# Deformable convolution by halves: 4x4 sampling tiles on the two row halves of TensorE in place of 7x7 tiles on its four column groups

## The chip, the core and the metric

The kernel runs on one core of a Trainium2 chip. The metric is the device time of one execution in microseconds, the median of several runs. Engines are called by the profile's names: PE is TensorE (PEld its weight loads), DVE is VectorE, ACT is ScalarE, POOL is GpSimd, SP is SyncE, which here only issues DMAs.

## The reference

The input is 32 images of 96 channels, 56 x 56, float32. Two layers follow each other. The first is an inverted bottleneck: a 1x1 convolution to 576 channels, a depthwise 3x3 convolution, a squeeze-and-excitation gate, a 1x1 projection back to 96 channels and the residual. The second computes attention over channels and positions from Fourier magnitudes (twice), a gate, an ordinary 3x3 convolution and a deformable 3x3 convolution, and normalises over the whole batch. The part that the change is about:

```python
y = x * ca * sa
offset = _conv(aux, off_w, off_b, (1, 1))          # 18 channels: 9 taps, x and y
gate = sigmoid(_conv(relu(_conv(aux, dg1_w, ...)), dg2_w, dg2_b))
y_base = _conv(y, base_w, base_b, (1, 1))
off = offset.reshape(b, 9, 2, h, w)
px = xx + off[:, :, 0]
py = yy + off[:, :, 1]
sampled = _grid_sample_taps(y, px, py)             # bilinear, 9 samples a position
y_def = einsum('bcthw,oct->bohw', sampled, def_w) + def_b
z = (1 - gate) * y_base + gate * y_def
zn = batch_norm(z)                                 # mean and variance over the batch
out = relu(zn + x)
```

## The kernel before

All 32 images go through both layers in one software pipeline (`layers`). While the main loop works on the deformable part of image b, two generators ("streams") are stepped beside it: `attend` of image b+1 (projection, Fourier transforms, attention) and `hidden` of image b+2 (the 1x1 and depthwise convolutions, the latter nine VectorE instructions a unit at line 223). `pump()` counts slots, and steps each stream as often as its share of the slots is due; things that wait are put in `later` with a slot number. The framework's scheduler then orders the instructions on each engine at build time; on SP the order is that of the program text. [...]

The main loop goes over bands of rows. Before, a band is 7 rows (`TR`), 8 bands an image, 256 in all, and a band is 8 sampling tiles of 7 x 7 positions (`TP` = 49). Sampling is done as a matmul: offsets reach at most 2 pixels (`REACH`), so a tile's samples come from a window of 11 x 11 = 121 pixels (`NS`), and the samples of all channels are the window's pixels (channels as the stationary operand, transposed to 121 partitions) times a matrix of bilinear weights, 121 x 441 (9 taps x 49 positions). Should an offset be larger, `gather_block` does everything again by gathering; it does not run on this input.

For each band the steps, with their lines, are:

- `offsets` (a generator, run two bands ahead, one `next` a slot): the joint convolution (L540: hidden gate, offsets and 32 base channels in one), ACT moves `off` out (L585), the base convolution for the other 64 channels (L569, two halves of the columns side by side) and its sum on DVE (L572); DVE takes the largest offset `top` (L591), POOL adds the place in the window (L593) and stores `od` to DRAM (L595); SP loads it back repeated as `ht` (L600); ACT and DVE make one-dimensional hat weights of it (L603, L605); POOL stores them as `hd` (L609).
- `weights_load` (L617, L619): SP loads column weights `wc` and row weights `wr` for two tiles, repeated over the window's partitions; `weights` (L625): DVE multiplies them. `AHEAD` and `READY` set how far ahead.
- `block_pixels` (L633): POOL copies the 8 windows `ybl` of the next band; `block_channels` (L643, L645): PE transposes each to 121 partitions, ACT copies it out as `yt`.
- `sample_tile` (L654, L660, L662): per tile, three matmuls of 32 channels each over the first 7 taps (343 columns) to partitions 0-31, 32-63, 64-95, and three for the last two taps to partitions 96-127, packed so that a later matmul can use all 128 rows; ACT copies the whole 128 x 343 to `v`.
- `gate_of` (L677), `deform` (L669): 7 matmuls over a band's 392 positions, the first on 96 rows, the other six on 128 (a full tap and a third of one of the last two taps); `combine` (L695 to L698) on DVE mixes with the base convolution; `store` (L945) on POOL.

Of the streams, the change touches the projection: `project_loads` (L271, L274) issues five `hq` loads and one residual load `xc` on POOL for a band of 7 rows, `project` (L283, L285) multiplies them. PSUM is 7 banks in a shared pool `mm` and one, `acc`, for small things.

Of the kernel before, what the change touches and what calls it, by code (L numbers as in the profile page):

```python
# [19 lines left out]
NCH = 5  # L20
# [10 lines left out]
TR = 7  # L31
NBD = H // TR
NTX = W // TR
TP = TR * TR
BW = TR * W
REACH = PD
SB = TR + 2 * REACH
# [5 lines left out]
VC = KA * TP  # L43
# [6 lines left out]
GP = 98  # L50
# [7 lines left out]
AHEAD = 2  # L58
READY = 2
# [84 lines left out]
def expand(nc, p, xts, unit):  # L144
# [23 lines left out]
    if half is None:  # L168
        nc.vector.memset(h1[:64, 0, :], 0.0)
        nc.vector.memset(h1[64:, HH + 1, :], 0.0)  # L170
        for r in range(1, HH + 1, TR):
            piece([(0, 0), (64, 1)], r, TR)
            yield
        piece([(0, 0)], HH + 1, 1)
        piece([(64, 1)], 0, 1)
        yield
    else:
        r = 1 - half
        for rows in (TR + 1, TR, TR, TR):
            piece([(0, half)], r, rows)  # L180
            r += rows
            yield
# [80 lines left out]
def project_loads(nc, p, x, h2d, q):  # L263

    half, n0 = divmod(q * BW, HB)
    terms = [(u, ch, slice(0, 128)) for u, (ch, hf) in enumerate(UNITS) if hf == half]
    terms.append((4, 4, slice(64 * half, 64 * half + 64)))
    rows = []
    for u, ch, ps in terms:
        hq = p["hq"].tile([128, BW], FP, name="hq")  # L270
        nc.gpsimd.dma_start(hq[ps], h2d[u, ps, n0 : n0 + BW])  # L271
        rows.append((ch, ps, hq))
    xr = p["xc"].tile([C, BW], FP, name="xc")
    nc.gpsimd.dma_start(xr, x[:, q * TR : (q + 1) * TR].rearrange("c h w -> c (h w)"))  # L274
    return rows, xr


def project(nc, p, rows):
# [3 lines left out]
    for i, (ch, ps, hq) in enumerate(rows):  # L282
        nc.tensor.matmul(pt[:C, :BW], w3s[ps, ch], hq[ps], start=(i == 0), stop=(i == NCH - 1))  # L283
    o = p["o"].tile([C, BW], FP, name="o")
    nc.scalar.activation(o, pt[:C, :BW], AF.Identity, bias=w["sh3"], scale=w["inv3"])  # L285
# [97 lines left out]
def attend(tc, p, b, x, h2d, pooled, x1, given=False):  # L383
# [7 lines left out]
    if not given:  # L391
        yield from squeeze(nc, p, pooled)
        rows, xr = project_loads(nc, p, x, h2d, 0)
        for _ in range(2):
            yield
        for q in range(NBD):
            o = project(nc, p, rows)
            yield
            nc.gpsimd.tensor_tensor(o, o, xr, ALU.add)
            nc.gpsimd.dma_start(x1[:, q * BW : (q + 1) * BW], o)  # L400
            if q + 1 < NBD:
                rows, xr = project_loads(nc, p, x, h2d, q + 1)
            yield
# [112 lines left out]
def load_rows(nc, p, yp, b, x1, r0, r1):  # L516
# [3 lines left out]
    sab = p["q2"].tile([C, TR, W], FP, name="sab")[:, : r1 - r0]  # L520
# [13 lines left out]
def conv3(nc, out, weights, yp, channels, j):  # L534

    view = out.rearrange("p (h w) -> p h w", h=TR)
    for k in range(NTAP):
        dy, dx = divmod(k, 3)
        r0 = j * TR + dy + PD - 1
        nc.tensor.matmul(view, weights[:, k], yp[:channels, r0 : r0 + TR, dx + PD - 1 : dx + PD - 1 + W],  # L540
# [13 lines left out]
def joint_conv(nc, p, yp, j):  # L554
# [11 lines left out]
    for k in range(NTAP):  # L566
        dy, dx = divmod(k, 3)
        r0 = j * TR + dy + PD - 1
        nc.tensor.matmul(pb[k % 2 * BC : (k % 2 + 1) * BC, :BW].rearrange("p (h w) -> p h w", h=TR), w["base"][:, k],  # L569
                         yp[:C, r0 : r0 + TR, dx + PD - 1 : dx + PD - 1 + W], start=(k < 2), stop=(k > NTAP - 3))  # L570
    nc.scalar.activation(yb[:BC], pb[:BC, :BW], AF.Identity, bias=w["cv"]("base_b")[:BC])
    nc.vector.tensor_tensor(yb[:BC], yb[:BC], pb[BC:, :BW], ALU.add)  # L572


def offsets(nc, p, yp, j, top, hids, ybs, hds):
# [8 lines left out]
    off = p["off"].tile([NOFF, NTX, TP], FP, name="off")  # L584
    nc.scalar.activation(off.rearrange("o t (r c) -> o t r c", r=TR),  # L585
                         pa.rearrange("o (r t c) -> o t r c", r=TR, t=NTX), AF.Identity, bias=w["offc"])
    yield
    for _ in joint:
        pass
    flat = off.rearrange("o t p -> o (t p)")  # L590
    nc.vector.tensor_reduce(top, flat, AX.X, ALU.max, apply_absolute_value=True)  # L591
    yield
    nc.gpsimd.tensor_tensor(off, off, w["place"].unsqueeze(1).to_broadcast([NOFF, NTX, TP]), ALU.add)  # L593
    od = p["dp"].tile([NTX, NOFF, TP], FP, name="od")
    nc.gpsimd.dma_start(od.rearrange("t o p -> o t p"), off)  # L595
    yield
    yield
    ht = p["ht"].tile([NTX * SB, 2 * KP], FP, name="ht")
    src = od.rearrange("t o p -> t (o p)").unsqueeze(1).to_broadcast([NTX, SB, 2 * KP])
    nc.sync.dma_start(ht, src)  # L600
    yield
    yield
    nc.scalar.activation(ht, ht, AF.Abs, bias=w["blk"])  # L603
# [3 lines left out]
    hd = p["dp"].tile([SB, 2, NTX, KP], FP, name="hd")  # L607
    for x in range(2):
        nc.gpsimd.dma_start(hd[:, x].rearrange("i t n -> t i n"), ht[:, x * KP : (x + 1) * KP])  # L609
# [3 lines left out]
def weights_load(nc, p, hd, m):  # L613

    src = hd.rearrange("i x t n -> i x (t n)")[:, :, 2 * m * KP : 2 * (m + 1) * KP]
    wc = p["wc"].tile([NS, 2 * KP], FP, name="wc")
    nc.sync.dma_start(wc, src[:, 0].unsqueeze(0).to_broadcast([SB, SB, 2 * KP]))  # L617
    wr = p["wr"].tile([NS, 2 * KP], FP, name="wr")
    nc.sync.dma_start(wr, src[:, 1].unsqueeze(1).to_broadcast([SB, SB, 2 * KP]))  # L619
# [9 lines left out]
def block_pixels(nc, p, yp, j):  # L629

    yb = p["ybl"].tile([C, NTX, SB, SB], FP, name="ybl")
    for t in range(NTX):
        nc.gpsimd.tensor_copy(yb[:, t], yp[:C, j * TR : j * TR + SB, t * TR : t * TR + SB])  # L633
    return yb


def block_channels(nc, p, yb):

    yt = p["yt"].tile([128, NTX, C], FP, name="yt")
    for i in range(0, NTX, 4):  # L640
        pt = bank(p)
        for t in range(4):
            nc.tensor.transpose(pt[:NS, t * C : (t + 1) * C], yb[:, i + t].rearrange("c r x -> c (r x)"),  # L643
                                p["w"]["ident"][:C, :C])
        nc.scalar.copy(yt[:NS, i : i + 4].rearrange("p t c -> p (t c)"), pt[:NS, : 4 * C])  # L645
# [3 lines left out]
def sample_tile(nc, p, yt, s, v, n):  # L649


    ps = bank(p)
    for i in range(3):
        nc.tensor.matmul(ps[i * QC : (i + 1) * QC, :VC], yt[:NS, n, i * QC : (i + 1) * QC], s[:, :VC],  # L654
                         start=True, stop=True)

    for i in range(3):
        lo = TP + i * 2 * TP if i else 0
        hi = TP + (i + 1) * 2 * TP
        nc.tensor.matmul(ps[3 * QC :, lo:hi], yt[:NS, n, i * QC : (i + 1) * QC], s[:, KP - (hi - lo) :],  # L660
                         start=True, stop=True)
    nc.scalar.copy(v[:, n], ps[:, :VC])  # L662


def deform(nc, p, pd, v):

    for k in range(KA):
        ks = slice(0, 128 if k else C)
        nc.tensor.matmul(pd[:C, :BW].rearrange("c (r t x) -> c t r x", r=TR, t=NTX), p["w"]["def"][ks, k],  # L669
                         v[ks, :, k * TP : (k + 1) * TP].rearrange("c t (r x) -> c t r x", r=TR),  # L670
# [176 lines left out]
def layers(tc, a, dp, x1d, zd, stats, far):  # L847
# [8 lines left out]
    with ExitStack() as ctx:  # L856
        p = {"dp": ctx.enter_context(tc.tile_pool(name="l1d", bufs=3, space=DRAM))}
        pools(tc, ctx, p, PSUM, (("mm", 7), ("acc", 1)))
# [5 lines left out]
        pools(tc, ctx, p, None, (("xt", 2), ("acch", 2), ("pl", 2), ("w3s", 1), ("hq", 9), ("o", 2), ("x2", 3),  # L864
                                 ("ca", 2), ("s1p", 1), ("xc", 2), ("sp", 1), ("sq", 1), ("q1", 1), ("q2", 2), ("hid", 3), ("yb", 4),
# [481 lines left out]
```

## Time and profile before

| | before |
|---|---|
| median of 3 runs | 11,224.36 us (11,204.04 to 11,231.37) |
| profiled execution | 11,185.3 us |
| its span, first to last instruction | 11,183.5 us |
| mean granted TensorE clock | 0.896 |
| busy PE / DVE / POOL / ACT | 9478.8 / 7817.4 / 4841.1 / 4418.5 us |
| DMA | 1,941.96 MB in 1,072,677 packets |

The busy shares are averages over the whole span: a prologue up to about 480 us, the main loop, and the final normalisation after 10,767 us. Groups of instructions carry a line and the names of their tiles, `out<-in`; PE and DMA have to be read with the timeline, since matmuls overlap and a busy time is not a rate. A wait names the engine that waited, its line, what it waited for, the sum in us, how often and the longest.

### The profile page before, as it was taken

To read this page: it belongs to the slowest core of one execution; us is meant where nothing else is said; L and a number is where in the kernel's file an instruction comes from. 1 tells how busy PE (TensorE), PEld (TensorE's weight loads), DVE (VectorE), ACT (ScalarE), POOL (GpSimd) and SP (SyncE) were. 2 spreads that over 40 slices of the span, in tenths; PEclk is the share of its full clock that TensorE was granted. 3 is DMA by queue.
4 is the path that set the end of the run, shared out by engine and by line. 5 is a ranking of instruction groups with operands and counts; after the bars stand their busy time and mean duration, and the time that the engine had idled before them with its cause. 6 is when DMAs were issued, how large, how long until landed. Compare 5 with 4: busy or idle time off the path is not lost. (4 is left out here: it accounts for less than half of the span.)

```text
span 11183.5 us, 142158 instructions
## 1 busy us (share of the span) xinstructions
PE 9478.8 (85%) x52806; PEld 4985.0 (45%) x52806; DVE 7817.4 (70%) x7490; ACT 4418.5 (40%) x8007; POOL 4841.1 (43%) x5934
## 2 busy tenths in 40 slices
PE   2688989899899899999998998998899898989940
PEld 1344444444444444444444444444444444444520
DVE  7677777777777777777776777777777777776322
ACT  1344444444444434444443444444344443433322
POOL 1254544544444445445444444444544444444200
PEclk7789999999999999999999999989999999999965
DMA  1455666665555666556666655556665565566569
GB/s 64 121 164 169 181 175 178 182 178 176 168 174 174 177 177 179 169 171 175 177 179 178 175 172 167 175 169 175 180 178 166 175 179 169 176 178 177 156 204 287
DMA packets 1072677, 1941.96 MB, mean 174 GB/s; under 512 B 637930, under 2 KB 643770, under 8 KB 1062759
## 3 DMA queue, kind: packets, MB, share of 16 engines
q1 hardware_dynamic: 844082, 1187.45, 37.3%
q0 software_dynamic: 179168, 473.36, 15.0%
q10 hardware_dynamic: 48725, 271.96, 6.8%
q8 instruction: 420, 6.88, 0.3%
q14 instruction: 282, 2.31, 0.1%
HBM read 1497.75 MB, written 434.32 MB: 173 GB/s over the span
## 5 line engine op out<-in xcount | busy, mean ns | idle before, releaser
L223 DVE SCALAR_TENSOR_TENSOR acch<-hp,w,acch 128x1568 f32<-128x1568 f32 (+1 forms) x2304 | 4325.2, 1881 | 47.9 <-ACT hp L164 33.7
L633 POOL COPY ybl<-yp 96x121 f32<-96x121 f32 x2048 | 1689.2, 871 | 666.2 <-PE mm L643 666.2
L625 DVE TENSOR_TENSOR wc<-wc,wr 121x882 f32<-121x882 f32 x1024 | 1132.5, 1108 | 1072.2 <-DMA wr<-hd 1024.1
L540 PE MATMUL mm<-yp,c_jointW 101*128 101x392 f32 x4608 | 1740.1, 525 | 90.2 <-DMA yp<-fqd 90.1
L654 PE MATMUL mm<-wc,yt 121*32 121x343 f32 x12288 | 1611.6, 481 | 211.2 <-DVE yb L572 101.1
L660 PE MATMUL mm<-wc,yt 121*32 121x98 f32 (+1 forms) x12288 | 1561.9, 272 | 0.0
L669 PE MATMUL mm<-v,c_def 128*96 128x392 f32 (+1 forms) x3584 | 1381.7, 538 | 102.4 <-ACT v L662 102.4
L160 PE MATMUL mm<-xt,w 96*128 96x392 f32 (+3 forms) x2688 | 1164.5, 570 | 160.3 <-ACT hp L164 98.9
L540 PEld LDWEIGHTS mm<-yp,c_jointW 101*128 101x128 f32 x4608 | 889.8, 199 | 789.0 <-issue 264.7
L283 PE MATMUL mm<-hq,w3s 128*96 128x392 f32 (+1 forms) x2560 | 1055.3, 552 | 217.2 <-DMA hq<-h2d 186.2
L660 PEld LDWEIGHTS mm<-wc,yt 121*32 121x32 f32 x12288 | 1136.5, 112 | 81.8
L609 POOL DMA_DIRECT2D hd<-ht x512 | 323.8, 635 | 1698.1 <-DVE ht L605 1358.9
L271 POOL DMA_DIRECT2D hq<-h2d x1280 | 723.4, 569 | 579.2 <-DMA h2d<-acch 267.2
L164 ACT ACTIVATE hp<-mm,sh,inv 128x392 f32<-128x392 f32 (+2 forms) x1216 | 813.6, 672 | 375.3 <-PE mm L160 236.4
L662 ACT COPY v<-mm 128x343 f32<-128x343 f32 x2048 | 874.4, 442 | 186.5 <-PE mm L660 125.3
L669 PEld LDWEIGHTS mm<-v,c_def 128*96 128x96 f32 (+1 forms) x3584 | 610.3, 177 | 705.0 <-issue 595.6
L569 PE MATMUL mm<-yp,c_base0W 96*64 96x392 f32 x4608 | 912.3, 502 | 0.0
L205 ACT ACTIVATE acch<-acch,sh,inv 128x1568 f32<-128x1568 f32 x288 | 487.4, 1692 | 1071.2 <-DVE acch L223 1070.6
L593 POOL TENSOR_TENSOR off<-off,c_place 18x392 f32<-18x392 f32 x256 | 410.4, 1603 | 1073.6 <-DVE top L591 1073.6
L654 PEld LDWEIGHTS mm<-wc,yt 121*32 121x32 f32 x12288 | 380.4, 110 | 1008.9 <-issue 510.2
L283 PEld LDWEIGHTS mm<-hq,w3s 128*96 128x96 f32 (+1 forms) x2560 | 414.7, 178 | 732.8 <-issue 457.2
L605 DVE TENSOR_SCALAR ht<-ht 88x882 f32<-88x882 f32 x256 | 187.8, 734 | 717.8 <-ACT ht L603 717.5
(190 smaller groups left out, 10744.7 us busy)
## 6 DMA issues: line engine op xcount, KB each, us to landing
wc<-hd SPq DMA_DIRECT2D x1024, 416.9 KB
wr<-hd SPq DMA_DIRECT2D x1024, 416.9 KB
h2d<-acch ACTq DMA_DIRECT2D x288, 784.0 KB
hq<-h2d POOLq DMA_DIRECT2D x1024, 196.0 KB, 6.4
ht<-od SPq DMA_DIRECT2D x256, 303.2 KB
hd<-ht POOLq DMA_DIRECT2D x512, 151.6 KB, 6.8
x<-x1d SPq DMA_DIRECT2D x768, 98.0 KB
xt<-in_x SPq DMA_DIRECT2D x64, 609.0 KB
```

The costliest lines, as they stand in the source:

```text
L160: nc.tensor.matmul(pt[p0 : p0 + w1.shape[1], : rows * W], w1, xts[hf][:, r0 * W : (r0 + rows) * W], start=True, stop=True)
L164: nc.scalar.activation(h1[lo:hi, row0 : row0 + rows, 1 : 1 + W], pt[lo:hi, : rows * W].rearrange("p (h w) -> p h w", h=rows), AF.Silu, bia ...
L223: nc.vector.scalar_tensor_tensor(acc[:, lo:hi], win, wk, acc[:, lo:hi], ALU.mult, ALU.add)
L283: nc.tensor.matmul(pt[:C, :BW], w3s[ps, ch], hq[ps], start=(i == 0), stop=(i == NCH - 1))
L540: nc.tensor.matmul(view, weights[:, k], yp[:channels, r0 : r0 + TR, dx + PD - 1 : dx + PD - 1 + W], start=(k == 0), stop=(k == NTAP - 1))
L569: nc.tensor.matmul(pb[k % 2 * BC : (k % 2 + 1) * BC, :BW].rearrange("p (h w) -> p h w", h=TR), w["base"][:, k], yp[:C, r0 : r0 + TR, dx + ...
L625: nc.vector.tensor_tensor(wc, wc, wr, ALU.mult)
L633: nc.gpsimd.tensor_copy(yb[:, t], yp[:C, j * TR : j * TR + SB, t * TR : t * TR + SB])
L654: nc.tensor.matmul(ps[i * QC : (i + 1) * QC, :VC], yt[:NS, n, i * QC : (i + 1) * QC], s[:, :VC], start=True, stop=True)
L660: nc.tensor.matmul(ps[3 * QC :, lo:hi], yt[:NS, n, i * QC : (i + 1) * QC], s[:, KP - (hi - lo) :], start=True, stop=True)
L662: nc.scalar.copy(v[:, n], ps[:, :VC])
L669: nc.tensor.matmul(pd[:C, :BW].rearrange("c (r t x) -> c t r x", r=TR, t=NTX), p["w"]["def"][ks, k], v[ks, :, k * TP : (k + 1) * TP].rearr ...
```

## The change

A band is now 8 rows, 7 bands an image (224 in all), and is worked on in two halves of 28 columns. The sampling tile is 4 x 4 positions with a window of 8 x 8 = 64 pixels, so two tiles, one above the other, fill 128 partitions: a pair shares one transpose, and its two sampling matmuls (96 channels, 9 taps x 16 = 144 columns) use the lower and the upper 64 rows of TensorE and write to two PSUM banks. A half has 7 pairs, sampled in two goes: pairs 0 to 2 into two banks, pairs 3 to 6 into four. ACT copies all nine taps to partitions 0-95 of `v`; the last two taps reach partitions 96-127 by three DMAs on ACT's queue (`pack`). The deformable matmuls of a half are issued after the first go of the next half, into a PSUM bank of their own; `combine` follows two slots after the second half.

Around it: the shared PSUM pool has 6 banks; weight loads are one half ahead, four per half on 64 partitions each; the windows of a half are two POOL copies; the place is added into a tile of its own (`at`) and no longer waits for `top`; `hd` is stored by four DMAs a band; the sum of the base convolution comes a step later, more steps lie between `ht`'s load and its use, and `attend_rows` comes four slots after its loads; the projection keeps bands of 7 rows (`ER`), its `hq` loads are on SP and two bands ahead, with 8 buffers for 9.

```diff
+ER = 7
+EW = ER * W
+NBD = H // RB
+BW = NBW
+TS = 4
+NTX = W // TS
+NTH = NTX // 2
+TP = TS * TS
+GROUPS = ((0, 3),), ((3, 5), (5, 7))
-SB = TR + 2 * REACH
+SB = TS + 2 * REACH
-AHEAD = 2
-READY = 2
+AHEAD = 1
+READY = 1
...
 def project_loads(nc, p, x, h2d, q):
...
-        nc.gpsimd.dma_start(hq[ps], h2d[u, ps, n0 : n0 + BW])
+        nc.sync.dma_start(hq[ps], h2d[u, ps, n0 : n0 + EW])
...
+        rows = [project_loads(nc, p, x, h2d, q) for q in range(2)]
...
+            xr = residual_load(nc, p, x, q)
+            o = project(nc, p, rows.pop(0))
             yield
+            if q + 2 < H // ER:
+                rows.append(project_loads(nc, p, x, h2d, q + 2))
             nc.gpsimd.tensor_tensor(o, o, xr, ALU.add)
...
 def offsets(nc, p, yp, j, top, hids, ybs, hds):
...
+    yield
+    yield
+    next(joint)
+    at = p["off"].tile([NOFF, NTX, 2, TP], FP, name="at")
+    nc.gpsimd.tensor_tensor(at.rearrange("o t s p -> o (t s) p"), off.rearrange("o t s p -> o (t s) p"),
+                            w["place"].unsqueeze(1).to_broadcast([NOFF, 2 * NTX, TP]), ALU.add)
+    od = p["dp"].tile([NTX, 2, NOFF, TP], FP, name="od")
+    nc.gpsimd.dma_start(od.rearrange("t s o p -> o (t s) p"), at.rearrange("o t s p -> o (t s) p"))
+    yield
+    yield
+    next(joint, None)
+    nc.vector.tensor_reduce(top, off.rearrange("o t s p -> o (t s p)"), AX.X, ALU.max, apply_absolute_value=True)
+    yield
+    yield
+    ht = p["ht"].tile([NTX * SB, 4, KP], FP, name="ht")
+    src = od.rearrange("t s o p -> t (s o p)").unsqueeze(1).to_broadcast([NTX, SB, 4 * KP])
+    nc.sync.dma_start(ht.rearrange("q n k -> q (n k)"), src)
+    for _ in range(4):
+        yield
...
+def block_channels(nc, p, yp, j, h):
+    yt = p["yt"].tile([2 * NS, NTH, C], FP, name="yt")
+    yb = p["ybl"].tile([C, NTH, 2, SB, SB], FP, name="ybl")
+    src = yp[:C, j * RB : j * RB + SB, h * NTH * TS : h * NTH * TS + SB]
+    for s in range(2):
+        blocks = bass.AP(src.tensor, src.offset + s * TS * WY, [src.ap[0], [TS, NTH], [WY, SB], [1, SB]])
+        nc.gpsimd.tensor_copy(yb[:, :, s], blocks)
+    for lo, hi in ((0, 4), (4, NTH)):
+        pt = bank(p)
+        for t in range(lo, hi):
+            nc.tensor.transpose(pt[:, (t - lo) * C : (t - lo + 1) * C], yb[:, t].rearrange("c s r x -> c (s r x)"),
+                                p["w"]["ident"][:C, :C])
+        nc.scalar.copy(yt[:, lo:hi].rearrange("p t c -> p (t c)"), pt[:, : (hi - lo) * C])
+    return yt
...
+def sample_tiles(nc, p, yt, s, v, group):
+    pts = [(bank(p), bank(p)) for _ in group]
+    for (lo, hi), pt in zip(group, pts):
+        for t in range(lo, hi):
+            for k in range(2):
+                ps = slice(k * NS, (k + 1) * NS)
+                nc.tensor.matmul(pt[k][:C, (t - lo) * KP : (t - lo + 1) * KP], yt[ps, t], s[ps, t * KP : (t + 1) * KP],
+                                 start=True, stop=True)
+    for (lo, hi), pt in zip(group, pts):
+        for k in range(2):
+            nc.scalar.copy(v[:C, :, lo:hi, k].rearrange("c k t p -> c t k p"),
+                           pt[k][:C, : (hi - lo) * KP].rearrange("c (t k p) -> c t k p", t=hi - lo, k=NTAP))
+
+def pack(nc, v):
+    for i in range(3):
+        nc.scalar.dma_start(v[C:, 1 + 2 * i : 3 + 2 * i], v[i * QC : (i + 1) * QC, KA:])
+
+def deform(nc, p, pd, v, h):
+    out = pd[:C, :BW].rearrange("c (q w) -> c q w", q=RB)[:, :, h * W // 2 : (h + 1) * W // 2]
+    for k in range(KA):
+        ks = slice(0, 128 if k else C)
+        nc.tensor.matmul(out.rearrange("c q (t x) -> c t q x", x=TS), p["w"]["def"][ks, k],
+                         v[ks, k].rearrange("c t s (r x) -> c t (s r) x", r=TS),
+                         start=(k == 0), stop=(k == KA - 1))
...
-        pools(tc, ctx, p, PSUM, (("mm", 7), ("acc", 1)))
+        pools(tc, ctx, p, PSUM, (("mm", 6), ("acc", 1), ("pd", 1)))
...
+            for h in range(2):
+                v = p["vp"].tile([128, NTAP, NTH, 2, TP], FP, name="v")
+                prepare(2 * n + h + READY + AHEAD)
+                s = ready.pop(0)
+                yt = yts.pop(0)
+                for i, group in enumerate(GROUPS):
+                    sample_tiles(nc, p, yt, s, v, group)
+                    for _ in range(group[0][0], group[-1][1]):
+                        next(more, None)
+                        pump()
+                    if i == 0:
+                        for end in ends:
+                            end()
+                        ends.clear()
+                        if h == 1 and n + 1 < len(bands):
+                            yts.append(block_channels(nc, p, yp, bands[n + 1][1], 0))
+                        ready.extend(weights(nc, *ws) for ws in loads[:1])
+                        del loads[:1]
+                        if h == 0:
+                            yts.append(block_channels(nc, p, yp, j, 1))
+                pack(nc, v)
```

## The prediction

> **What bounds the kernel now.** I read the shares of the page first, then the same shares by stretches of the loop, then who TensorE waited for, then its timeline. The page:
>
> ```profile
> PE 9478.8 (85%) x52806; PEld 4985.0 (45%) x52806; DVE 7817.4 (70%) x7490; ACT 4418.5 (40%) x8007; POOL 4841.1 (43%) x5934
> ...
> PE   2688989899899899999998998998899898989940
> ...
> PEclk7789999999999999999999999989999999999965
> ```
>
> TensorE is full from about 480 us (prologue) to 10,767 us (after it only `normalise`, bound by DMA, which the change does not touch). The stretches of 3200 us show how full: PE 2884 of 3200 us busy, clock 0.92. The clock is either whole or halved, so 0.92 means half speed for about 16% of the time. TensorE's waits between 500 and 10,200 us sum to some 926 us. The largest:
>
> ```profile
> PE mm L283 <- DMA hq<-h2d: 169.6, 37, 9.6
> PE mm L336 <- POOL x L316: 134.9, 59, 9.2
> PE acc L376 <- DVE m_fy L373: 133.4, 28, 7.1
> PE mm L654 <- DVE yb L572: 100.5, 34, 5.7
> ...
> PE mm L654 <- ACT o L285: 74.5, 26, 4.1
> PE mm L669 <- ACT v L662: 72.1, 29, 4.8
> ```
>
> Only the first (output-projection input) and the last three (a PSUM bank not yet emptied, samples not yet copied) touch the change. No other engine is near full. So work taken off TensorE is time, unless it returns as waits. What the work costs is read in the timeline (start, length, engine, line):
>
> ```profile
> 5023.29 0.49 PE L654 MATMUL mm<-wc,yt 121*32 121x343 f32 x3
> 5023.31 0.52 PE L660 MATMUL mm<-wc,yt 121*32 121x147 f32 x3
> ...
> 5041.88 1.09 PE L643 MATMUL mm<-c_ident,ybl 96*121 96x96 f32 x8
> 5042.80 4.83 PE L669 MATMUL mm<-v,c_def 96*96 96x392 f32 x14
> 5047.48 2.79 PE L283 MATMUL mm<-hq,w3s 128*96 128x392 f32 x8
> ...
> 5149.48 1.05 PE L336 MATMUL mm<-c_FU,x 112*112 112x116 f32 x8
> 5150.37 0.83 PE L160 MATMUL mm<-xt,w 96*128 96x392 f32 x2
> ```
>
> Start to start: 14 deformable instructions take 4.68 us, 334 ns for 392 columns (a float32 matmul is two instructions). The eight of the Fourier transform take 0.89 us with the first weight load; after it starts are 99 ns apart for 116 columns, so a load of 112 weight columns hides behind as little as that. Through both: 0.851 ns a column. Transposes start 106 ns apart[...]. The three L654 start 7 ns apart: four column tiles run together, and a 7x7 tile costs 2 x 343 x 0.851 = 0.58 us.
>
> [...] two sampling tiles between two L160 (5061.44 to 5063.62) take 2.18 us where 0.67 of L160 and 1.16 of sampling add to 1.83: 0.35 us a visit. [...] no row tiles run side by side in the trace of before. [...] copies L633 take 277 to 10,565 ns, median 291, mean 871. [...] `zd` and `od` land a median 2.3 us after issue.
>
> **The change, part by part.** TensorE, at whole clock:
> - Sampling. Gone: 2048 tiles x 0.58 = 1188 us. New: 3136 pairs, each two matmuls of 144 columns on the two row halves, 2 x 144 x 0.851 = 0.246 us if they overlap: 771 us. The changed instruction order has 1026 visits to sampling against 1523: 174 us less at 0.35. Sum -591.
> - Transposes: 3136 x 0.112 (128 weight columns) = 351 against 2048 x 0.106 = 217: +134.
> - Deformable matmuls: 6272 x 0.193 = 1210 against 3584 x 0.334 = 1197: +13. The three convolutions per band keep their columns (7 x 448 = 8 x 392): 0.
> - Together -444 us, at clock 0.92 -483 us.
>
> What returns or goes as TensorE waits:
> - **The packing** is new: `pack` moves taps 7 and 8 from partitions 0-95 to 96-127 by three DMAs on ACT's queue (1344 x about 0.33 us, as L207's; ACT instructions behind it wait that long). Before, matmuls wrote those partitions. Deformable matmuls from the second on wait for it, and everything behind them on TensorE. Laying the changed order end to end at the durations above, the second comes a median 6.2 us after its half's last sampling matmul. Over 448 halves the shortfall sums to 146 us if the rows need 4 us, 260 at 5, 428 at 6, 647 at 7, 873 at 8. They need the last copies (about 1.2), issue (0.33), landing between 2.3 (`zd`) and 6.4 (`hq`): 3.9 to 7.9. I take 5, and 200 us, as the real loop runs slower than this count. Ends 0 and 870.
> - **hq loads** (1280, about 569 ns each on POOL) move to SP (L311's take 448 ns there) and come two bands ahead, limited by 8 buffers for two sets of 5: SP stands at the fourth or fifth load until the next projection, with weight, `ht` and `x` loads behind it. Wait now 170 us in the loop; I take -150. Ends -300 (with half-clock time after long gaps) and +50.
> - **PSUM**: 6 shared banks instead of 7 (deform gets its own), and a second go takes four at once. Copies: 896 x 518 + 1792 x 395 ns = 1172 us against 874, from the slope of 343 columns (442 ns) to 464 (545). The base-convolution bank is held a slot longer for VectorE. I take +50; ends -100 and +300.
> - **Block copies**: 14 windows of 8x8 in two POOL instructions per half, behind `at`/`od` of the same band, ahead of the transposes. POOL's queue also gets 896 `hd` issues for 512 (+384 x 0.63 = 242 us) and `od` in rows of 64 bytes for 196, and loses the 1280 of hq. Estimate from L633: 0.6 us each unblocked, 1.2 blocked. `at` no longer waits for VectorE's `top` (1073.6 us of POOL waits now). I take 0, hidden behind the base convolution (3.8) and deform (2.7). Uncovered: up to 3 us on 224 bands, half of it seen, +300; a gain is excluded, as TensorE waits for no copy now.
>
> VectorE loses 1024 products of 1108 ns for 448 of about 1.26 us (-568) and some `ht` work; it is off the path. But it waits 1024 us for `wr`, and lead from load to product falls from three slots of about 4 us to three of 2.7; the bytes halve (874 MB to 462 MB): taken as 0, ends -50 and +150. The longer delays in slots (`attend_rows`, `ht`) and the gather-path edits (no such line runs) are nothing: they move waits off queues.
>
> Sum: -483 + 200 - 150 + 50 = -383 us against the profiled execution, 11,185.3 us (span 11,183.5): 10,802. The median of the runs is 11,224.4, 39 above it: **10,840 us**.
>
> **Rivals.**
> 1. The forecast, 10,840; for it, TensorE's fullness. Chance 0.55.
> 2. Waits clear as well: hq -300, banks -100, packing 50: -833, 10,390. For it, POOL is freed of hq issues. Against it, most waits have other causes. Chance 0.10.
> 3. Work goes, but the in-order queues of ACT, VectorE and SP set the pace: ACT stood 1070 us on `acch` and 760 us on `ht`, and stray copies behind such a wait now hold more banks. Banks at +300 and products at +150: -383 + 250 + 150 = +17 at worst, half of it -180: 11,040 to 11,240. Chance 0.12, a third of it no change.
> 4. **Slower by the packing.** One transfer behind h2d stores of 784 KB on the same ring, and ACT instructions between copy and issue. Gain without packing is 583; shortfall passes this just below 7 us from last matmul to landed rows. At 8 us: -583 + 873 = +290, 11,510. Against it: the `zd` landing. Chance 0.15.
> 5. The change doesn't do what it says: the row halves run one after the other, 0.49 us a pair. Then 771 us more at 0.92 is +838: 11,680. Against it: column tiles overlap. Chance 0.08.
>
> **How the numbers follow.** 0.3% (34 us) is about what a measurement of this kernel tells from no change. Faster: 0.55 + 0.10 + 0.08 = 0.73; same 0.04; slower 0.15 + 0.08 = 0.23. Range 10,430 to 11,430: it leaves out rival 5, about half of 4 and some of 2, some 0.19. The likeliest case alone spans 10,600 to 11,050.
>
> **What would show it.** Right: pairs of sampling matmuls starting a few ns apart in the two halves and 246 ns from pair to pair; TensorE's busy share down, not up; a new wait of deformable matmuls on a DMA of `v`, 100 to 350 us; the hq wait small; VectorE's products near 565 us. Wrong: pairs 490 ns apart (rival 5); `v` waits over 600 us (rival 4); large waits of L283's, sampling's or transposes' successors on ACT copies, or on the block copies of POOL.

## The result and the profile after

The changed kernel takes 11,066.85 us in the median (11,042.67 to 11,084.23) against 11,222.05 for the kernel before beside it: 0.9862 (95% interval 0.9839 to 0.9885), 1.4% faster, where 3.4% were forecast. The profiled execution took 11,071.8 us (before: 11,185.3). Its page, TensorE's share, its slices and its clock:

```profile
PE 9203.3 (83%) x43334; PEld 5237.1 (47%) x43334; DVE 7356.0 (66%) x6658; ACT 4596.4 (42%) x9063; POOL 3396.4 (31%) x3758
...
PE   2698988888889888888988888898889889888830
...
PEclk7788999889989998888889899889988989898865
```

TensorE's busy time fell, as forecast, but the 9s of the slices became 8s and the clock's row has 8s that were 9s. The groups (line, engine, operation, count | busy us, mean ns | idle before, by what) say where:

```profile
L689 PE MATMUL pd<-v,c_def 128*96 128x224 f32 (+1 forms) x6272 | 1682.8, 421 | 568.0 <-DMA v<-v 548.3
L652 POOL COPY ybl<-yp 96x448 f32<-96x448 f32 x896 | 1010.2, 1152 | 2039.1 <-PE mm L656 2029.0
L641 DVE TENSOR_TENSOR wc<-wc,wr 128x1008 f32<-128x1008 f32 x448 | 570.0, 1272 | 769.7 <-DMA wr<-hd 572.8
```

The deformable matmuls waited 548 us for the packing (`DMA v<-v`), 200 in the forecast. VectorE's products and GpSimd's copies are as sized. TensorE's waits between 500 and 10,000 us (total, times, longest):

```profile
PE pd L689 <- DMA v<-v: 482.4, 133, 9.6
PE mm L670 <- DVE yb L581: 101.2, 59, 3.0
PE mm L290 <- DMA hq<-h2d: 82.1, 29, 5.2
PE acc L455 <- ACT c L452: 69.7, 29, 3.9
...
PE mm L656 <- POOL ybl L652: 30.6, 27, 1.4
...
PE mm L343 <- POOL x L323: 6.2, 8, 3.4
PE acc L383 <- DVE m_fy L380: 5.2, 13, 0.5
```

One wait is new and large. Two that the change was not thought to touch, `x` by GpSimd and `m_fy` by VectorE (268 us before), are all but gone. The sampling runs nearly as forecast (start, length):

```profile
5000.80 0.74 PE L656 MATMUL mm<-c_ident,ybl 96*128 96x96 f32 x7
5001.47 1.22 PE L670 MATMUL mm<-wc,yt 64*96 64x144 f32 x16
5002.63 3.70 PE L290 MATMUL mm<-hq,w3s 128*96 128x392 f32 x10
```

Sixteen instructions, four pairs on two row halves, in 1.16 us to the next start; one after the other, at the forecast's 0.851 ns a column, they would take 1.96, an estimate.

To set gain against loss I summed TensorE's records and the granted clock in the trace over the loop, from 480 us to the end of the last deformable matmul: busy time weighted by the clock ("work at whole clock"), idle time, and what busy time lost to the half clock. The clock's records hold two values in both traces, 1.0 and 0.5; in the changed kernel's, instructions of the joint convolution start 381 ns apart in the middle at 1.0 and 747 at 0.5, transposes 82 and 160. In us:

| kernel | loop | work at whole clock | idle | lost to half clock | time at half clock |
|---|---|---|---|---|---|
| before | 10,289 | 8,613 | 1,009 | 667 | 1,638 |
| after | 10,178 | 8,104 | 1,177 | 897 | 2,140 |
| e1, without packing | 9,389 | 8,089 | 650 | 650 | 1,382 |
| e2, late deformable matmuls | 9,618 | 8,236 | 737 | 644 | 1,410 |
| e15, before with half the products | 9,952 | 8,640 | 808 | 505 | 1,150 |

TensorE lost 509 us of work; 168 us of idle time and 230 us of half clock took most of it back.

### The profile page after: what moved, and what is told of

Same layout as the page of the kernel before. It is cut to its first block, busy times and chain, and to the rows that moved or that the text cites. A ratio compares the mean times of both kernels' runs of the same rounds, so it can differ in the third digit from the quotient of the medians.

```text
span 11069.9 us, 124049 instructions
## 1 busy us (share of the span) xinstructions
PE 9203.3 (83%) x43334; PEld 5237.1 (47%) x43334; DVE 7356.0 (66%) x6658; ACT 4596.4 (42%) x9063; POOL 3396.4 (31%) x3758
## 5 line engine op out<-in xcount | busy, mean ns | idle before, releaser
L689 PE MATMUL pd<-v,c_def 128*96 128x224 f32 (+1 forms) x6272 | 1682.8, 421 | 568.0 <-DMA v<-v 548.3
L652 POOL COPY ybl<-yp 96x448 f32<-96x448 f32 x896 | 1010.2, 1152 | 2039.1 <-PE mm L656 2029.0
L548 PE MATMUL mm<-yp,c_jointW 101*128 101x448 f32 x4032 | 1629.9, 556 | 0.4 <-DMA yp<-fqd 0.3
L689 PEld LDWEIGHTS pd<-v,c_def 128*96 128x96 f32 (+1 forms) x6272 | 1161.4, 194 | 978.6 <-DMA v<-v 604.2
L670 PE MATMUL mm<-wc,yt 64*96 64x144 f32 x12544 | 1250.2, 316 | 192.2 <-DVE yb L581 103.7
L163 PE MATMUL mm<-xt,w 96*128 96x392 f32 (+3 forms) x2688 | 1153.8, 570 | 128.3 <-ACT hp L167 80.5
L670 PEld LDWEIGHTS mm<-wc,yt 64*96 64x96 f32 x12544 | 952.7, 172 | 572.3 <-issue 253.0
L674 ACT COPY v<-mm 96x288 f32<-96x288 f32 (+1 forms) x2688 | 1003.2, 441 | 391.2 <-PE mm L670 351.4
L641 DVE TENSOR_TENSOR wc<-wc,wr 128x1008 f32<-128x1008 f32 x448 | 570.0, 1272 | 769.7 <-DMA wr<-hd 572.8
L577 PE MATMUL mm<-yp,c_base0W 96*64 96x448 f32 x4032 | 905.1, 550 | 0.0
L364 PE MATMUL mm<-s,c_GV 112*112 112x464 f32 x1536 | 717.4, 612 | 9.3 <-ACT hp L167 7.7
L163 PEld LDWEIGHTS mm<-xt,w 96*128 96x128 f32 (+1 forms) x2688 | 384.0, 189 | 553.1 <-issue 358.1
```

The costliest lines, as they stand in the source:

```text
L163: nc.tensor.matmul(pt[p0 : p0 + w1.shape[1], : rows * W], w1, xts[hf][:, r0 * W : (r0 + rows) * W], start=True, stop=True)
L364: nc.tensor.matmul(pt[: 2 * W, :n].rearrange("p (q u) -> p q u", q=NPB), w["GV"][:, g], m, start=(k == 0), stop=(k == 1))
L641: nc.vector.tensor_tensor(wc, wc, wr, ALU.mult)
L652: nc.gpsimd.tensor_copy(yb[:, :, s], blocks)
L670: nc.tensor.matmul(pt[k][:C, (t - lo) * KP : (t - lo + 1) * KP], yt[ps, t], s[ps, t * KP : (t + 1) * KP], start=True, stop=True)
L674: nc.scalar.copy(v[:C, :, lo:hi, k].rearrange("c k t p -> c t k p"), pt[k][:C, : (hi - lo) * KP].rearrange("c (t k p) -> c t k p", t=hi - ...
```

## The experiments

My theory: the gain went into the packing, whose rows land later than the order of the work covers, and each such wait costs clock as well. The rivals: the queues would hold TensorE anyway; the issuing ScalarE is what is late; the clock falls for a reason of its own.

### How much the packing takes: e1

```diff
-                pack(nc, v)
```
`v` is two fixed tiles with rows 96 to 127 set to zero once.

> The three transfers that pack rows 96 to 127 of each half are left out (those rows stay zero), so the output is not the reference's; nothing else differs from the changed kernel (11,067 us). If the packing is what took the gain (548 us of waits at the deformable matmuls), 10,420 to 10,620 us, no wait of TensorE on v over 50 us, half-clock time no higher than before. If the in-order queues would hold TensorE in its place anyway, other waits (weight products, PSUM, the reads h2d) grow by about what goes and the time stays above 10,870 us.

Measured: 10,273.56 us, 0.9142 of before (0.9125 to 0.9160): 793 us less than the changed kernel, more than expected. ScalarE's 1,344 issues, 0.57 us each in the mean, went too. TensorE's waits, the largest:

```profile
PE acc L249 <- ACT acch L208: 89.2, 29, 4.6
PE mm L290 <- DMA hq<-h2d: 86.0, 34, 4.0
PE acc L455 <- ACT c L452: 77.0, 28, 5.4
PE mm L343 <- ACT yt L658: 73.5, 26, 5.2
```

None took the packing's place, so the rival of the queues falls. Against after, the table has 527 us less idle time and 247 us less lost to half clock: **the packing costs its wait and, here, half as much again in clock**. It also shows that the rest of the change, with ScalarE free of those issues, is worth 953 us, not the 583 that the prediction's terms give without packing.

### Is it the cover? e2 and e9

```diff
-                    if i == 0:
+                    if i == 1:
                         for end in ends:
                             end()
                         ends.clear()
+                    if i == 0:
```
`end` issues the deformable matmuls of the half before. They come after the second go and its steps (e2), or right behind the second go's sampling matmuls (e9).

> The deformable matmuls of a half are put after the second go of the next half instead of the first, some 10 us later; the packing is as it was. If what counts is that the packed rows land about 8 us after the last sampling matmul while 5 us of other work lies between, the wait on v falls below 150 us and the time is 10,520 to 10,770 us. If the loss lies in ScalarE standing at the packing transfers, or in the order of the queues, TensorE finds another wait in its place and the time stays above 10,900 us.

> The deformable matmuls of a half right after the second go's sampling matmuls of the next half, ahead of the steps of the other stages that follow that go (the late order puts them behind those steps). If the packing costs what its rows are late by, laid against the cover of the order, the trace of the kernel without packing and the landing times of the late order give 45 to 105 us of wait on v here (700 to 770 us for the order of the changed kernel), and 10,430 to 10,560 us. If what the late order brings is not the cover but where the matmuls stand among the others, it lies halfway or worse: above 10,700 us.

Measured: e2 10,472.02 us, 0.9321 (0.9302 to 0.9339), with e7 below, which does not differ from it, **the fastest of the kernels that leave nothing out**; e9 10,539.39, 0.9404 (0.9371 to 0.9437). TensorE's waits in e2:

```profile
PE mm L670 <- DVE yb L581: 97.0, 31, 4.7
PE acc L383 <- DVE m_fe L380: 93.4, 30, 5.7
PE mm L290 <- DMA hq<-h2d: 89.1, 43, 5.4
PE pd L689 <- DMA v<-v: 75.6, 50, 3.8
```

and in e9 the one in question:

```profile
PE pd L689 <- DMA v<-v: 52.2, 51, 3.6
```

The 45 to 105 us expected of e9 come from a sum over the 448 halves: landing time less cover, where positive. The same sum gave 700 to 770 us for the order of the changed kernel, whose wait is 482 (548 over the whole span): right for one order, too high for the other. Its size fits the landing of all rows of a half, and TensorE waits for the first. Of the 548 us, 541 end at the first matmul that needs packed rows, in the middle 0.04 us after the semaphore of the first of the three transfers completes; the other two transfers account for 7. By these semaphores the first rows are there 6.8 us in the mean after the last sampling matmul of their half, in e2 as in the changed kernel, and all three sets after about 9 us in both. Nothing lands earlier; only what lies between changed, and the theory of the cover stands. The late order also costs something: its work at whole clock is 132 us above the changed kernel's, 126 of it in sampling, which is begun 1,302 times in place of 1,133. Waiting later is what paid here: 76 us of wait on `v` in e2 for 482.

### Is it the queue that issues? e3, e8, e10, e11, e12

```diff
-        nc.scalar.dma_start(v[C:, 1 + 2 * i : 3 + 2 * i], ...)
+        nc.gpsimd.dma_start(v[C:, 1 + 2 * i : 3 + 2 * i], ...)                          # e3; e8 with e2
+        nc.sync.dma_start(...)                                                          # e10, with e2
+        (nc.scalar, nc.sync, nc.gpsimd)[i].dma_start(...)                               # e11; e12 with e2
```

> The three packing transfers are issued by GpSimd instead of ScalarE. If ScalarE's standing (each issue waits for an earlier transfer and holds the copies and activations behind it) makes the rows late and also delays other work, the wait on v falls below 250 us and the time is 10,620 to 10,820 us. If only the landing time of the transfers matters, the wait on v is 450 us or more and the time 11,000 to 11,150 us. If GpSimd's queue is too full (block copies and its own transfers behind the packing), it is slower than 11,150 us.

> The late deformable matmuls with the packing issued by GpSimd. ScalarE is relieved of its standing at the packing transfers while the later rows (GpSimd took up to 15 us) have some 10 us more cover. If ScalarE's standing is what delays the copies and activations that TensorE now waits for (hp, gate, acch: 160 us of waits), 10,300 to 10,430 us. If GpSimd's queue is what suffers (its own transfers and additions behind the packing), 10,490 to 10,650 us.

> The late deformable matmuls with the packing issued by SyncE. If ScalarE's issues (0.5 us each, and its standing at earlier transfers) are what delays hp, gate and acch, 10,280 to 10,420 us and those waits (160 us) fall by half. If SyncE's other transfers (hq, x of x1d, the weight columns) come late behind the packing, which waits for ScalarE's copies, 10,490 to 10,700 us with new waits on hq or x.

> The changed kernel with its order kept and one of the three packing transfers on each of ScalarE, SyncE and GpSimd. If the rows are late because three issues stand in one queue (first issue to third 2.5 us in the middle, up to 6.6), the last rows land near 6 us instead of 8 after the last sampling matmul, and by the table of the prediction the time falls by 300 to 450 us: 10,620 to 10,770 us. If each queue brings a wait of its own (the last of the three counts), 10,950 to 11,250 us.

> The late deformable matmuls with one packing transfer on each of the three queues. If the remaining wait on v (76 us) and ScalarE's standing are what is left of the packing, each queue bearing a third, 10,330 to 10,440 us. If, as with all three on GpSimd (10,576) or on SyncE (10,571), the other queues' own work is delayed by more than ScalarE gains, 10,480 to 10,580 us.

| packing issued by | order of the change | late order (e2) |
|---|---|---|
| ScalarE | 11,067, 0.9862 | 10,472, 0.9321 |
| GpSimd | e3: 11,193, 0.9965 (0.9948 to 0.9981) | e8: 10,576, 0.9425 (0.9407 to 0.9443) |
| SyncE | | e10: 10,571, 0.9435 (0.9403 to 0.9467) |
| one each | e11: 10,752, 0.9598 (0.9563 to 0.9634) | e12: 10,569, 0.9415 (0.9389 to 0.9441) |

ScalarE does stand behind the packing in the changed kernel: between 500 and 10,000 us it was idle for 264 us until transfers of `v` had landed. The largest of these waits:

```profile
ACT o L292 <- DMA v<-v: 134.3, 25, 8.4
```

But moving it helps only where the order gives no cover, and there only when spread. On GpSimd the wait on `v` grew:

```profile
PE pd L689 <- DMA v<-v: 721.9, 142, 15.2
```

The first of its transfers took 4.9 us from issue to landing in the middle, like ScalarE's; it was issued later, 3.2 us in the mean after the last sampling matmul for ScalarE's 1.9. e11 met its time, but not its reason. Its rows landed in the mean 5.4 (ScalarE), 8.2 (SyncE) and 7.6 us (GpSimd) after the last sampling matmul, and the last of the three after 10.5, later than in the changed kernel. Yet the wait on `v` fell from 482 to 309 us and the time at half clock from 2,140 to 1,703. The waits by transfer show where: the rows of the first are there 1.4 us earlier, and over the whole span TensorE's waits for them fell from 541 to 158 us, while those for the third rose from 2 to 161. Whether they come earlier because ScalarE stands less was not separated. In the late order each other queue costs about 100 us: e10's waits on `yb`, `hp` and `xt` are 208, 152 and 74 us (e2: 97, 74, 34). There all three expected gains failed. Idle time and half clock do not go together here: against the same order with ScalarE issuing, e3, e8, e10 and e12 have 146 to 255 us more idle time in the loop and 26 to 188 us less lost to half clock.

### The clock: e4, e7, e5

Some 20 stretches of 17 to 31 us, in about two of three images, run at half clock, nearly all of them with TensorE busy throughout. One, by the timeline:

```profile
5459.09 0.32 PE L455 MATMUL acc<-c,c_cp 24*96 24x1 f32 x2 [3.60 <-ACT c L452]
...
5478.27 0.81 PE L490 MATMUL acc<-s,tv 56*56 56x56 f32 x6
5479.01 0.80 PE L670 MATMUL mm<-wc,yt 64*96 64x144 f32 x4
...
5486.10 4.43 PE L548 MATMUL mm<-yp,c_jointW 101*128 101x448 f32 x6
```

It starts at a wait for the relu of the channel attention and ends near the joint convolution.

```diff
-    nc.scalar.activation(c1, pc[: 2 * MID, 0:1], AF.Relu, bias=w["cp1b"])
+    nc.vector.tensor_scalar(c1, pc[: 2 * MID, 0:1], w["cp1b"], 0.0, ALU.add, ALU.max)
```

> The relu of the channel attention (24 x 1) that TensorE waits 2.8 to 3.6 us for, once an image, is done by VectorE instead of ScalarE. If the long stretches at half clock (about 18 of 20 to 30 us) begin with this wait and then stay because the small matmuls and the 64-row sampling pairs don't bring the clock back, they mostly vanish: time at half clock from 2,140 us to under 1,800 us, kernel 10,850 to 10,990 us. If the clock is lost in gaps everywhere alike, or another wait of the same chain starts the stretch, 11,030 to 11,075 us and the stretches stay.

> The late deformable matmuls and the relu on VectorE together. If the two are separate (a wait on the rows; the start of a long stretch at half clock), their gains add: 10,472 less about 40, so 10,410 to 10,450 us. If in the late order that wait no longer stands alone, no change: 10,460 to 10,490 us.

Measured: e4 11,025.90 us, 0.9806 (0.9768 to 0.9844); e7 with the late order 10,468.67, 0.9321 (0.9303 to 0.9339), no change from e2. In e4 the wait is gone and the long stretches fall from 20 to 12, but time at half clock only from 2,140 to 2,086 us, and a wait of L163 on `yt` (73 us) takes its place. Neither theory's numbers were met, and its interval touches that of the changed kernel. e1 keeps 20 long stretches, so they are not the packing's. But the kernel before has only two, 41 us together for 481 in the changed kernel: the rest of the change brought them. By half of the difference they cost up to 220 us, an estimate; the prediction has no term for it.

e5 measures the clock by itself: eight stages before the first image, each behind a wait.

```diff
+        stage(60, [(all, m, 0)], 224)                    # 128 rows
+        stage(76, [(lo, m, 0), (hi, m, 0)], 144)         # pairs of 64 rows
+        stage(96, [(lo, m, 0)], 144)                     # 64 rows, one half
+        stage(30, [(slice(0, 96), m, 0)], 448)           # 96 rows
+        ...                                              # 96 x 224, 121 x 343, 56 x 448, 56 x 56
```

> The changed kernel with eight added stages before its first image, each some 40 to 60 us of one kind of matmul back to back behind a wait of TensorE of over 10 us (their results are not used): 128 rows; pairs of 64 rows on both halves; 64 rows on one half; 96 rows with 448 columns moving; 96 rows with 224; 121 rows in column tiles of 32; 50-odd rows with 448; 56 rows with 56. If the clock comes back only on windows in which most of the array's rows work (the theory of the long stretches), the 128, 121 and 96 row stages reach the whole clock after 3.4 to 10 us, while the 64-row and 56-row ones stay at half for their whole length; for the 64-row pairs too, if two matmuls on two halves count no more than one. If any back-to-back work brings the clock back, all eight stages reach it within 10 us.

The middle of each stage in the view by stretches; the column before the last two is the granted clock:

```profile
100.00:120.00 20.00, 20.00 (x107) 17.23 (x107) 0.00 (x0) 0.00 (x0) 0.00 (x0) 1.00 0.00 1
138.00:154.00 16.00, 16.00 (x266) 16.00 (x264) 0.00 (x0) 0.00 (x0) 0.00 (x0) 1.00 0.01 2
170.00:214.00 44.00, 44.00 (x185) 44.00 (x184) 0.00 (x0) 0.00 (x0) 0.00 (x0) 0.50 0.00 1
233.00:253.00 20.00, 20.00 (x54) 8.52 (x53) 0.00 (x0) 0.00 (x0) 0.00 (x0) 1.00 0.00 0
...
345.00:388.00 43.00, 43.00 (x59) 15.90 (x57) 0.00 (x0) 0.00 (x0) 0.00 (x0) 0.50 0.00 0
403.00:430.00 27.00, 27.00 (x291) 26.90 (x289) 0.00 (x0) 0.00 (x0) 0.00 (x0) 0.50 0.01 2
```

128, 96 and 121 rows, and pairs of 64, reached the whole clock 2.8 to 4.9 us after the stage began. 64 rows on one half and 56 rows stayed at half clock for all of their 46, 45 and 28 us, TensorE busy at every moment. So my theory held for matmuls of few rows and failed for the pairs. The stretches in the kernel fit it where matmuls of 56 rows lie between short pieces of others. The kernel before has the same matmuls of 56 rows and hardly a long stretch, so they alone do not make one; what part the pairs, cut short there, have in it was not tried.

### Where the rest of the gain is from: e6, e13 to e17, in the kernel before

Of the other 370 us (953 less 583) most is idle time. In the table it fell by 359 us from before to e1, where the forecast's hq and PSUM terms make 100; work and clock together fell by 541, where the forecast had 483. That makes 317 us; the rest lies between these two profiled executions and the medians. Four parts of the change were tried in the kernel before, alone or in pairs:

```diff
 e6:   -nc.gpsimd.dma_start(hq[ps], h2d[...])        +nc.sync.dma_start(hq[ps], h2d[...])    # two groups ahead
 e13:  -for t in range(NTX): nc.gpsimd.tensor_copy(yb[:, t], ...)
       +nc.gpsimd.tensor_copy(yb, bass.AP(src.tensor, src.offset, [src.ap[0], [TR, NTX], [WY, SB], [1, SB]]))
 e14:  e6 and e13
 e15:  -tensor_tensor(wc, wc, wr, ALU.mult)          +tensor_tensor(wc[:, :KP], wc[:, :KP], wr[:, :KP], ALU.mult)
 e16:  -nc.gpsimd.tensor_tensor(off, off, place, ALU.add)   +nc.gpsimd.tensor_tensor(at, off, place, ALU.add)
       -("off", 2)                                   +("off", 1)      # buffers of each tile, as in the change
 e17:  e15 and e16
```

> The kernel before with one part of the change alone: the reads hq of h2d issued by SyncE, two row groups ahead, instead of GpSimd one ahead. By the prediction's term this is worth 150 us: 11,050 to 11,130 us, wait on hq under 40 us. If SyncE's queue makes the reads wait behind its other transfers (as the changed kernel suggests, whose wait on hq is still 82 us), 11,120 to 11,180 us. If another wait takes its place, 11,190 to 11,250 us.

> The kernel before with GpSimd's eight block copies a band made as one copy of 96 x 968, alone. If the waits that the changed kernel lost without the prediction naming it (x by GpSimd 132 us, hq 170, m_fy 133, the reads of x1d and fqd 151) hung on GpSimd's full queue, 10,900 to 11,080 us and these waits fall by half or more. If the copies were covered, as the prediction had it (0 us), 11,190 to 11,250 us.

> The kernel before with both: the single block copy and hq read by SyncE two groups ahead. If GpSimd's queue is relieved by both alike, 60 to 150 us below the copies alone. If hq on SyncE gains nothing by itself (alone it was 0.3% slower), within 30 us of the copies alone or above it.

> The kernel before with VectorE's weight products made over the first half of their columns only (the other half of the weights stays the column factor alone, so the output is not the reference's); VectorE is spared some 550 us, about what the change spares it. If the waits that the changed kernel lost beside the packing (x by GpSimd, m_fy, hq, fqd: 520 us in the trace before) hung on VectorE's share, 10,900 to 11,100 us. If the products were covered, as the prediction had it (0 us), 11,180 to 11,240 us.

> The kernel before with the additions of the place (GpSimd) written to a tile of their own, so that they no longer wait for VectorE's maximum of the offsets; GpSimd stood 1,074 us at that wait, with hq's issues and the products of x queued behind it. If that standing is what made x and hq late, 10,950 to 11,120 us, with both waits halved. If not, 11,190 to 11,240 us.

> Both of the last two in the kernel before (output not the reference's, as in the first). If each takes part of the same waits, a little below the better of the two; if the idle time came neither from VectorE's products nor from GpSimd's standing but from the order of the stages over the bands (seven bands of two halves instead of eight), 11,170 to 11,240 us like the two alone.

| | us | ratio to before (interval) |
|---|---|---|
| e6 hq by SyncE | 11,250.87 | 1.0031 (1.0014 to 1.0047) |
| e13 one block copy | 11,237.32 | 1.0020 (1.0009 to 1.0032) |
| e14 both | 11,290.40 | 1.0070 (1.0047 to 1.0093) |
| e15 half the products | 10,839.47 | 0.9649 (0.9631 to 0.9668) |
| e16 separate `at` | 11,221.99 | 0.9992 (0.9979 to 1.0006) |
| e17 e15 and e16 | 11,243.76 | 1.0008 (0.9998 to 1.0019) |

hq alone is no gain: its wait grew from 170 to 259 us, in 123 pieces for 37.

```profile
PE mm L287 <- DMA hq<-h2d: 258.6, 123, 8.3
```

The block copies alone shorten GpSimd's group from 1,689 to 456 us, and no wait of TensorE follows: they were covered. Half of the products (VectorE's group 1,132 to 667 us) is worth 392 us by itself, of which the table has 201 as idle time and 162 as half clock; in e15 two waits that no edit touches fell with it, from 133 and 132 us:

```profile
PE acc L376 <- DVE m_fy L373: 38.8, 26, 3.4
PE mm L336 <- POOL x L316: 38.5, 31, 7.2
```

But with `at` split, which alone changes nothing, the same relief is worth nothing: in e17 TensorE waits where e15 had 30 and 39 us:

```profile
PE mm L160 <- ACT sq L359: 171.7, 28, 8.1
...
PE mm L336 <- POOL x L316: 134.3, 32, 11.1
```

The single buffer of `off` is not what held e17: ScalarE rewrites it at the earliest 8.1 us after its last reader has ended. What follows is narrow: relief of VectorE can be worth 392 us here, and splitting `at` takes that away; why was not found. That the changed kernel's 370 us are from VectorE's relief is suggested by the two waits, which fall there as in e15, but not shown: the change splits `at` as well. This stays open.

## Why the prediction was wrong in size

- **TensorE's work, -444 us at whole clock: right**, -509 by the trace. Its parts are less even, taken from start to start: sampling -424 (forecast -591), transposes +78 (+134), deformable matmuls +44 (+13), and gate, joint convolution and the 1x1 convolution to 576 channels -177 together, where 0 stood. Of sampling the kernel before had less than reckoned: 1,463 us, where 1,188 and 1,523 visits at 0.35 us, an estimate from one place of the trace, make 1,721. That more weight columns slow a transpose (0.112 us with 128, for 0.106 with 121) was an estimate too, and wrong: at whole clock those with 128 start 82 ns apart, those with 121 106. The pairs overlap: in e5, with no other work between, instructions start some 61 ns apart, 0.245 us a pair (0.246 in the forecast). So matmuls on the two row halves ran side by side. Rival 5 falls.
- **The clock taken as 0.92 throughout: wrong.** It was a constant in the sum; it depends on the waits and on what is issued after them. Thirds of the loop have 0.90, 0.89 and 0.90 after and 0.93, 0.92, 0.92 in e1.

```profile
3700.00:6900.00 3200.00, 2841.62 (x13451) 1618.86 (x13450) 2235.83 (x1980) 1397.40 (x2805) 1070.49 (x1159) 0.89 0.51 139
```

```profile
3700.00:6900.00 3200.00, 2988.40 (x14449) 1692.04 (x14446) 2379.98 (x2128) 1509.48 (x3008) 1157.00 (x1250) 0.92 0.53 143
```

  The first line is of after, the second of e1. Of after's 248 falls to half clock in the loop, nine in ten follow 3.4 us (its shortest stretch at half clock is 3.41) in which TensorE was busy for under 56%. A gap of 1.5 to 2 us at whole clock was followed by a fall within 3.4 us in 43 of 75 cases, one of over 2 us in 171 of 173. Beside the constant, the forecast had half clock only after long gaps, as a part of hq's end of -300; of the 248 falls, 12 follow 3.4 us without any work of TensorE.
- **Packing, +200 us: the step that failed.** It was mis-sized, 200 us for the 793 of e1, in two ways. I took 5 us from the last sampling matmul to landed rows; the rows that TensorE waits for, those of the first transfer, are there after 6.8 us in the mean. Of these, 1.9 us pass until the first issue, where the forecast had 1.2 for the copies (in the middle 0.83, but with a long tail), and 4.9 from issue to landing, where its 5 us left 3.8. Between the 428 us that its table gives for 6 us and the 647 for 7, 6.8 us make some 600, an estimate; the trace has 548 of wait. And the term had nothing for the clock, 247 us against e1. That the table's 873 us for 8 us come near 793 is chance: they are a wait for the last rows, without the clock. The issues were mis-sized too, 0.51 us in the middle for 0.33 and three in one queue, 3.2 us in the mean from the first to the end of the third with waits between; but only 7 of the 548 us hang on the second and third.
- **hq, -150 us: wrong.** Alone it is +0.3%. The wait did fall from 170 to 82 us in the changed kernel; e6 does not have what made it fall.
- **PSUM, +50 us: not seen.** Waits of sampling matmuls for a bank to be emptied (`yb`, `o`, `hp` and `sq`) sum to 187 us before and 156 after, 31 less and inside the ends.
- **Block copies, 0: right.** 1.15 us each (1.2 in the forecast when blocked), 31 us of wait, and e13 shows them covered before as well. By blocked I meant a copy held up beside VectorE. In the trace of before, each of the 694 copies of 0.6 us and more (mean 2.0) shares over half of its time with VectorE instructions of two inputs (TENSOR_TENSOR, SCALAR_TENSOR_TENSOR); of the 1,354 shorter ones 336 do, and 915 meet none.
- **VectorE's products, 0: not safe.** The size was right (570 us, forecast 565). "Off the path" was read from their own waits; e15 gained 392 us, with the waits on `m_fy` and `x` 188 us shorter. The ends, -50 and +150, did not hold that.
- **The rivals.** Rival 4 had the mechanism, and a price near e1's by the chance just named, but set it against 583 us of gain where 953 were there, so it came out slower than before, and the kernel is faster. Two errors of opposite sign, 590 us in the packing and 370 in the rest, left the direction right: that is luck. Rival 3's numbers (11,040 to 11,240) hold the result without its mechanism: neither banks nor products waited more.
- **The signs named.** Pairs, lower busy share and products were seen; the hq wait halved, no more; the wait on `v` (548 us) was above the 350 named as right and just below the 600 named as wrong.

## What to carry to other kernels

Count a transfer between partitions from the last producer to the rows that the first consumer needs (here 6.8 us, not 5), and place the consumer behind that much other work before choosing another queue: moving seven matmuls by one go was worth over 5%, moving the issue less than 3% or a loss. A wait of some us on TensorE can cost more than its length, since the clock may halve after it, as it did here after 171 of 173 gaps of over 2 us: by the sums of the table, e1, e2, e11 and e15 regained 0.5 to 0.85 us of half clock with each us of idle time. It is no fixed rate: e3, e8, e10 and e12 go the other way, and from before to e1 359 us of idle time went with only 17 of half clock. And when a busy engine is relieved, look at who queues behind it, not only at the relieved instruction's own waits; test it in the order that will run, since the same relief was worth 392 us in one order and nothing in another.

## What was not expected of the hardware

- Matmuls of 56 rows, or of 64 on one half, did not bring back the whole clock in 28 to 46 us of unbroken work; 96 rows and more, and two halves of 64 together, did in 2.8 to 4.9 us (e5).
- Packing transfers within SBUF took ScalarE 515 ns to issue in the middle (the changed kernel), GpSimd 498 (e3) and SyncE 582 (e10), where the loads of `x` take SyncE 448 (before). GpSimd's went in 16 packets of 3,584 bytes a transfer, ScalarE's and SyncE's in 32 of 1,792.
- Transposes of 96 rows with 121 weight columns started 106 ns apart at whole clock and their weight loads took 186 ns (before); with 128 columns it was 82 and 140 ns (the changed kernel).
